# Four layers on one core: how the scan of Layer 0 gets its B and C, from four products with eightfold weights or from two products and a copy through DRAM

## The chip, the cores and the metric

The kernel runs on one core of a Trainium2 chip. The metric is the time of the device in microseconds (us). All values are 32-bit floats.

## The reference

The input x has 8 images of 128 channels and 64 x 64 positions. Four layers follow each other, each of the form x = x + f(group_norm(x)). Only Layer 0 is touched. It treats the lower 64 channels with a selective scan over the 4096 positions of an image (DI = 128 inner channels d, N = 16 states n, R = 4) and the upper 64 with a 3 x 3 convolution:

```python
xc = silu(conv1d(xs))                         # xs, z = layer_norm(t) @ in_w
dbc = xc @ xproj_w                            # 4 + 16 + 16 columns
dt = softplus(dbc[..., :R] @ dt_w + dt_b)
Bm = dbc[..., R:R + N]
Cm = dbc[..., R + N:]
dA = exp(dt[..., None] * A)
dBx = dt[..., None] * Bm[:, :, None, :] * xc[..., None]
h = dA_t * h + dBx_t                          # the scan, for each d and n
y = einsum('bdn,bn->bd', h, C_t)              # then y * silu(z) @ out_w, and x_hw's convolution beside it
```

Layer 1 sends rows over the image with a 9-tap convolution in four directions, each row depending on the one before. Layer 2 is three small convolutions, Layer 3 a deformable convolution with gathers.

## The kernel before

**Tiling of the scan.** For the scan a partition holds one pair (d, n): 8 channels d times 16 states n are 128 partitions. An image is cut into 4 chunks of 1024 positions (NCK), so there are 32 chunks in all, and each chunk into two halves h of T = 512. A half has 16 groups of 8 channels, taken two at a time, which makes 8 scan steps in a half, 16 in a chunk and 512 in all. In a step i (main loop, L639 on, with `where` L558):

- TensorE spreads u = dt * xc to the (d, n) partitions of the next step (`step_u`, `spread`, L568, bank u_ps) and dt, times A, for the step after it (`step_dt`, L568, bank dt_ps).
- ScalarE takes the exponential, the decay da (`step_decay`, L585).
- VectorE multiplies u_ps with B, which is tile bc[:, 0] (`step_scan`, L592), and scans twice (L603).
- ScalarE saves the last column (`step_carry`, L609), and GpSimd multiplies with C, tile bc[:, 1], in place (`step_weigh`, L614).
- In every odd step TensorE sums over n into ps_y (`round_sum`, L622), for the two steps three and two back. hb has four buffers, so a scan in an even step needs that sum of the step before.

**B and C.** Each (d, n) partition needs B or C of its n, the same for all eight d. `bc_product` (L446) gets this from TensorE directly: the weights w_bc (made once, L247) repeat the 16 columns of xproj_w eight times, so a product of 128 x 512 leaves B (i = 0) or C (i = 1) of one half on all 128 partitions, and ScalarE copies it into bc (L453). That is four products and four copies in a chunk. The tile bc has two buffers, one of a half each.

**Order of the work.** The schedule is written out by hand: every engine runs its instructions in the order in which the program issues them. The other work of a chunk c is planned in `plan_chunk` as events at step numbers relative to t0 = 16 c (L524 to L555). The steps below are counted modulo 16; an event can belong to the chunk before or after.

| step | events with work on TensorE (through the one bank "g" of `ps_g`) | other events |
|---|---|---|
| 0, 1 | xs_product (L395, three taps) | x_st load (even steps, in one chunk of four) |
| 2, 3 | bc_product (i = 0, 1) of half 1, then z_product (L407) | y_gate (step 2), silu (step 3, L412, with a table load before and after), x_o loads |
| 4 | y_product (L492, L494; evicted at L496) | |
| 5, 6 | v_product (L422) | normalize (step 5, L357), out_add with the x1d store, v_exp (step 6) |
| 7 | t_product (L365) | v_round (L430) |
| 8 | t_var (L373) | out_stats (L514) |
| 9 | | v_log |
| 10, 11 | bc_product of half 0 | v_sum and y_gate (step 10) |
| 12 to 15 | conv_taps (L477) | v_sum (step 14), load of xr (step 15) |

`ps_g` has one bank, so a product there waits until ScalarE has read the one before. SP issues nearly all loads and stores, in program order; it runs ahead of the steps until one of its transfers has to wait. In one chunk of four the group norms of an image are worked out as well (`norm_product`, L281 and L289, at steps 4 and 12).

**Layer 1 beside Layer 0.** The first four images go through Layer 1 while Layer 0 works on the last four: from step 280 on, the second of the two u_ps banks is given to Layer 1 (`shared`, L575), and from step 294 on each step also carries one row of it: nine taps on TensorE (L733, `layer1.products`) and one VectorE instruction (L741, `layer1.add`). After step 511 Layer 1 goes on alone, and Layers 2 and 3 follow.

Of the kernel before, what the change touches and what calls it, by code (L numbers as in the profile page):

```python
# [10 lines left out]
F32 = mybir.dt.float32  # L11
# [6 lines left out]
P = 128  # L18
# [4 lines left out]
GC, D, DI, N, R, KC = 64, 64, 128, 16, 4, 3  # L23
T = 512
# [10 lines left out]
def conv_preact_kernel(ctx: ExitStack, tc: tile.TileContext, a: dict, out: bass.AP):  # L35
    nc = tc.nc
    x_in = a["x"].rearrange("b c h w -> b c (h w)")
# [3 lines left out]
    dram = ctx.enter_context(tc.tile_pool(name="dram", bufs=1, space=DRAM))  # L41


    ident = const.tile([P, P], F32, name="ident")
    make_identity(nc, ident)

    gmat = const.tile([P, P], F32, name="gmat")
# [13 lines left out]
    x1d = [dram.tile([C, HW], F32, name=f"x1d{b}") for b in range(B)]  # L61
# [2 lines left out]
    x3d = [dram.tile([C, HW], F32, name=f"x3d{b}") for b in range(B)]  # L64
    tables = [dram.tile([SIDE * SX, 2 * C], F32, name=f"table{b}") for b in range(B)]


    norm1 = const.tile([P, B, 2], F32, name="norm1")

# [5 lines left out]
    xp = ctx.enter_context(tc.tile_pool(name="x", bufs=1))  # L75
    w1 = ctx.enter_context(tc.tile_pool(name="l1", bufs=2))
    X = xp.tile([P, HW, NB2], F32, name="X")
    layer0(tc, a, ident, gmat, x_in, x1d, norm1, Layer1First(tc, a, w1, x1d, norm1, X))

    with tc.tile_pool(name="l2w", bufs=1) as wp, tc.tile_pool(name="l2", bufs=2) as w2, tc.tile_pool(  # L80
        name="l3", bufs=2
    ) as w3, tc.tile_pool(name="l12ps", bufs=1, space=PSUM) as p2, tc.tile_pool(
        name="l3ps", bufs=2, space=PSUM
# [15 lines left out]
        N = two.TICKS  # L99
# [22 lines left out]
        for n in range(min(plans), (B + 1) * N):  # L122
            b, i = n // N - 1, n % N
# [19 lines left out]
    finish(tc, a, eps, od, x3d, y_out, st, const)  # L143


def layer0(tc, a, ident, gmat, x_in, x1d, norm1, layer1):

# [2 lines left out]
    nc = tc.nc  # L152
# [3 lines left out]
    with ExitStack() as ctx:  # L156
        wp = ctx.enter_context(tc.tile_pool(name="l0w", bufs=1))
        w2 = ctx.enter_context(tc.tile_pool(name="l0", bufs=2))
# [7 lines left out]
        def load(name, shape, *parts):  # L166
            t = wp.tile(shape, F32, name=name)
            for sl, src in parts:
                nc.sync.dma_start(t[sl], src)
            return t  # L170

        ALL, LO, HI = slice(0, P), slice(0, 64), slice(64, P)
# [4 lines left out]
        xproj_w = load("xproj_w", [DI, R + 2 * N], (ALL, a["xproj_w"]))  # L177
# [4 lines left out]
        ln_b = load("ln_b", [P, 1], *both(a["ln_b"]))  # L182
        in_b = load("in_b", [DI, 2], (ALL, a["in_b"]))
        c1_w = load("c1_w", [DI, KC], (ALL, a["conv1d_w"]))
        c1_rows = load("c1_rows", [P, KC * DI], (ALL, a["conv1d_rows"].to_broadcast([P, KC * DI])))
        c1_b = load("c1_b", [DI, 1], (ALL, a["conv1d_b"]))
        dt_b = load("dt_b", [DI, 1], (ALL, a["dt_b"]))
        d_ssm = load("d_ssm", [DI, 1], (ALL, a["D_ssm"]))
# [5 lines left out]
        with tc.manual_schedule():  # L194
# [5 lines left out]
            def ps_g(name):  # L200
                return pg.tile([P, T], F32, tag="g", name=name)
# [7 lines left out]
            ps = ps_g("ps_ec")  # L209
# [8 lines left out]
            ps = ps_g("ps_cb")  # L218
# [5 lines left out]
            ps = ps_g("ps_ib")  # L224
# [17 lines left out]
            ps = ps_g("ps_dt")  # L242
            nc.tensor.matmul(ps[:, 0:DI], lhsT=xdt_t, rhs=dt_w, start=True, stop=True)
            w_dt = wp.tile([DI, DI], F32, name="w_dt")
            nc.vector.tensor_copy(w_dt, ps[:, 0:DI])

            w_bc = wp.tile([DI, 2, 8, N], F32, name="w_bc")  # L247
            for i in range(2):
                nc.vector.tensor_copy(
                    w_bc[:, i], xproj_w[:, R + i * N : R + (i + 1) * N].unsqueeze(1).to_broadcast([DI, 8, N])  # L250
                )

            nc.scalar.activation(a_neg, a_neg, AF.Exp)
            nc.vector.tensor_scalar_mul(a_neg, a_neg, -1.0)
# [56 lines left out]
            def at(when, what):  # L311
                events.setdefault(when, []).append(what)
# [25 lines left out]
            def plan_chunk(c):  # L338
                b, g = c // NCK, c % NCK
                r0 = g * CR  # L340
                t0 = 16 * c
                s = S[c] = {}
# [100 lines left out]
                    nc.gpsimd.tensor_add(dt, w, s["rv"][:, h])  # L443
                    nc.gpsimd.tensor_mul(u, dt, s["xc"][:, h])

                def bc_product(i, h):  # L446
                    if i == 0:
                        s["bc", h] = w2.tile([P, 2, T], F32, name="bc")
                    ps = ps_g("ps_bc")
                    nc.tensor.matmul(  # L450
                        ps, lhsT=w_bc[:, i].rearrange("p d n -> p (d n)"), rhs=s["xc"][:, h], start=True, stop=True
                    )
                    nc.scalar.copy(s["bc", h][:, i], ps)  # L453

                def y_gate(h):
                    y = s["y", h] = w2.tile([DI, T], F32, name="y")
# [64 lines left out]
                def also(f, *args):  # L521
                    return lambda: f(*args)
# [10 lines left out]
                for h in range(2):  # L533
                    at(t0 - 16 + h, also(xs_product, h))
                    at(t0 - 14 + h, also(z_product, h))
                    at(t0 - 11 + h, also(v_product, h))
                    at(t0 - 6 + 4 * h, also(v_sum, h))
                    for i in range(2):
                        at(t0 - 6 + 8 * h + i, also(bc_product, i, h))
                    at(t0 + 10 + 8 * h, also(y_gate, h))  # L540
                    at(t0 + 11 + 8 * h, also(y_mul, h))
                at(t0 - 13, silu)
                at(t0 - 10, v_exp)
                at(t0 - 9, v_round)
                at(t0 - 8, v_rest)
# [88 lines left out]
            for c in range(total):  # L634
                plan_chunk(c)
                if c % NCK == 0:
                    plan_stats(c // NCK, 16 * c - 64)
# [641 lines left out]
```

## Time and profile before

| | |
|---|---|
| runs | 7735.23, 7738.29, 7739.29 us; median 7738.29 us |
| profiled execution, its own time | 7708.51 us |
| its span, first to last instruction | 7706.8 us |
| mean granted TensorE clock | 0.903 |
| busy: TensorE, VectorE, ScalarE, GpSimd | 81%, 58%, 45%, 52% of the span |
| L450 products of B and C | 256 records (two for a call), median 697 ns, overlapping |
| L453 copies | 128, median 586 ns |
| scan steps (L592), first and last start | 96.0 and 3101.8 us |

The profile is that of one execution, and each line of a timeline gives the start in us, the duration in us, the engine, the line of the kernel, the operation, the tiles (written <- read), the shapes and how many instructions were merged into the line. In brackets stands how long the engine was idle before it and what released it. A 32-bit matrix product appears as two records, each pair of them one call. PE is TensorE, DVE VectorE, ACT ScalarE, POOL GpSimd. In a row of the view of windows, each engine has its busy us and the number of instructions in brackets; PEclk is the granted TensorE clock as a share of full speed.

### The profile page before, as it was taken

What the parts mean: (1) busy time and instruction counts of PE and PEld (TensorE: products, weight loads), DVE (VectorE), ACT (ScalarE), POOL (GpSimd) and SP (SyncE); (2) the same over time, 40 slices, a digit from 0 to 9 for tenths busy, and PEclk for the clock granted to TensorE, in tenths of its full rate; (3) what the DMA queues carried; (4) which work ended last, traced back from release to release, by engine and by line L of the source; (5) the groups of instructions that cost most, each with busy time, mean ns of one, the idle gap of its engine ahead of it and who ended that gap; (6) DMA issues with size and microseconds to landing.
All of it is one profiled execution on the core that took longest, in us unless ns stands there. A gap on an engine that the chain in (4) does not pass through costs nothing.

```text
span 7706.8 us, 87506 instructions
## 1 busy us (share of the span) xinstructions
PE 6228.2 (81%) x30574; PEld 4062.3 (53%) x30574; DVE 4497.4 (58%) x5332; ACT 3460.5 (45%) x8218; POOL 4009.0 (52%) x3261
## 2 busy tenths in 40 slices
PE   6888878799999999859898898986678777776661
PEld 1222222255555556637677777775555555555550
DVE  4888889666566566141265666657545454555445
ACT  4555656433333332020155445455455555555552
POOL 3767777444444444000155555456566666666664
PEclk9988889699999999979999999998889888988785
DMA  1011111000000000041255556567666666666667
GB/s 43 27 38 36 39 34 38 31 11 27 12 29 21 9 15 15 12 157 29 66 182 183 166 174 192 167 186 253 204 210 202 208 194 208 201 206 203 186 185 264
DMA packets 333017, 897.81 MB, mean 116 GB/s; under 512 B 55464, under 2 KB 90544, under 8 KB 330528
## 3 DMA queue, kind: packets, MB, share of 16 engines
q0 software_dynamic: 184320, 604.13, 26.0%
q1 hardware_dynamic: 143648, 271.31, 10.6%
q10 hardware_dynamic: 4608, 16.78, 0.5%
q8 instruction: 242, 3.96, 0.2%
q14 instruction: 199, 1.63, 0.1%
HBM read 770.80 MB, written 121.21 MB: 116 GB/s over the span
## 4 chain that ended last, share of the span: by engine, by line
PE 62%; ACT 12%; DVE 8%; issue 8%; another core or an unknown queue 5%; DMA 3%; POOL 2%; SPq 0%; DVEq 0%; POOLq 0%; ACTq 0%
PE u_ps L733 13%; PE ps_l L733 10%; PE ps_s L1155 8%; PE ps_o L1166 6%; PE u_ps L568 5%; ACT X L1134 4%; PE ps_c L477 3%; PE ps_t L894 3%; DVE hb L603 3%; PE ps_y L622 3%; PE ps_x L395 3%; PE ps_t L908 2%; ACT samp L1106 1%; PE ps_off L990 1%
## 5 line engine op out<-in xcount | busy, mean ns | idle before, releaser
L614 POOL TENSOR_TENSOR hb<-hb,bc 128x1024 f32<-128x1024 f32 x512 | 1217.2, 2385 | 1279.7 <-ACT carry L609 893.5
L1123 POOL DMA_INDIRECT X<-table,idx x1386 | 1315.4, 949 | 788.4 <-issue 304.4
L1123 POOL DMA_INDIRECT got<-table,idx x918 | 878.6, 957 | 1351.4 <-DVE idx L1046 545.9
L603 DVE TENSOR_TENSOR_SCAN hb<-da,carry,u_ps 128x512 f32<-128x512 f32 x896 | 1097.8, 1266 | 251.0 <-PE ps_y L622 178.5
L585 ACT ACTIVATE da<-dt_ps 128x1024 f32<-128x1024 f32 x512 | 524.3, 1024 | 1337.7 <-PE dt_ps L568 1337.0
L1155 PE MATMUL ps_s<-ident,X 128*128 128x128 f32 x5544 | 829.7, 308 | 268.0 <-issue 175.7
L1141 DVE TENSOR_TENSOR X<-prod,X 128x768 f32<-128x768 f32 x462 | 442.4, 958 | 916.7 <-ACT X L1134 706.6
L1155 PEld LDWEIGHTS ps_s<-ident,X 128*128 128x128 f32 x5544 | 794.6, 221 | 339.3 <-issue 212.2
L1134 ACT ACTIVATE X<-X,wgt 128x128 f32<-128x128 f32 x2772 | 860.5, 394 | 0.0
L1166 PE MATMUL ps_o<-samp,dcn_w 128*128 128x256 f32 x2304 | 646.3, 422 | 225.3 <-ACT samp L1106 140.5
L568 PE MATMUL u_ps<-u,m_u 32*128 32x512 f32 x2048 | 629.6, 693 | 152.7 <-DVE hb L603 152.5
L1106 ACT COPY samp<-ps_s 128x384 f32<-128x384 f32 x768 | 360.9, 470 | 796.7 <-remote 479.9
L592 DVE TENSOR_TENSOR u_ps<-u_ps,bc 128x1024 f32<-128x1024 f32 x512 | 624.7, 1220 | 153.8 <-PE dt_ps L568 136.9
L568 PE MATMUL dt_ps<-dt,m_dt 32*128 32x512 f32 x2048 | 631.6, 695 | 17.5 <-ACT da L585 17.4
L1166 PEld LDWEIGHTS ps_o<-samp,dcn_w 128*128 128x128 f32 x2304 | 464.6, 212 | 332.9 <-ACT samp L1106 159.6
L1134 ACT ACTIVATE got<-got,wgt 128x128 f32<-128x128 f32 x1836 | 569.5, 393 | 0.0
L1139 DVE TENSOR_TENSOR prod<-X,prod 128x768 f32<-128x768 f32 x462 | 443.6, 960 | 100.6 <-ACT prod L1113 47.1
L741 DVE SCALAR_TENSOR_TENSOR X<-ps_l,X 128x256 f32<-128x256 f32 x252 | 106.2, 421 | 620.3 <-PE ps_l L733 473.4
L568 PEld LDWEIGHTS u_ps<-u,m_u 32*128 32x128 f32 x2048 | 164.8, 196 | 510.0 <-DVE hb L603 311.1
L741 DVE SCALAR_TENSOR_TENSOR X<-u_ps,X 128x256 f32<-128x256 f32 x252 | 106.9, 424 | 501.7 <-PE u_ps L733 501.3
L894 PE MATMUL ps_t<-xn,w 128*128 128x512 f32 (+4 forms) x688 | 305.2, 592 | 54.8 <-ACT t L901 22.5
L1155 PE MATMUL ps_s<-ident,got 128*128 128x128 f32 x2076 | 294.0, 287 | 38.2 <-issue 28.6
(227 smaller groups left out, 10393.2 us busy)
## 6 DMA issues: line engine op xcount, KB each, us to landing
table<-tok SPq DMA_DIRECT2D x128, 256.0 KB
x<-x1d SPq DMA_DIRECT2D x96, 256.0 KB
X<-table,idx POOLq DMA_INDIRECT x1386
x<-x2d SPq DMA_DIRECT2D x48, 384.0 KB
x3h<-x3d SPq DMA_DIRECT2D x16, 1056.0 KB
x_st<-in_x SPq DMA_DIRECT2D x64, 256.0 KB
x_o<-in_x SPq DMA_DIRECT2D x64, 256.0 KB
x1d<-res SPq DMA_DIRECT2D x64, 256.0 KB
```

The source lines that it names most:

```text
L568: nc.tensor.matmul(ps[:, j, :], lhsT=mask[q, r].rearrange("p d n -> p (d n)"), rhs=S[c][src, h][q, :], start=True, stop=True,)
L585: nc.scalar.activation(da, steps[i]["dt"], AF.Exp)
L592: nc.vector.tensor_mul(st["bc"], st["bc"], s["bc", h][:, 0].unsqueeze(1).to_broadcast([P, 2, T]))
L603: nc.vector.tensor_tensor_scan(hb[:, j, :], st["da"][:, j, :], st["bc"][:, j, :], start, ALU.mult, ALU.add)
L614: nc.gpsimd.tensor_mul(hb, hb, S[c]["bc", h][:, 1].unsqueeze(1).to_broadcast([P, 2, T]))
L733: nc.tensor.matmul(ps[:, c0:c1, :], lhsT=w[:, k, :], rhs=v[:, prev, c0 + k - PAD : c1 + k - PAD, :], start=(k == PAD), stop=(k == K - 1),)
L894: nc.tensor.matmul(ps[:, o0 - a0 : o1 - a0, :], lhsT=self.w1[:, k, :], rhs=S["xn", g][:, i0 + o0 : i0 + o1, :], start=(k == 2), stop=(k == 4),
L1123: nc.gpsimd.indirect_dma_start(out=got[:, k, :, :].rearrange("p q c -> p (q c)"), out_offset=None, in_=tab, in_offset=bass.IndirectOffsetO ...
L1134: nc.scalar.activation(got[:, k, q, :], got[:, k, q, :], AF.Identity, scale=wgt[:, t, k0 + k, q : q + 1])
L1139: nc.vector.tensor_mul(prod, got[:, :, 0:2, :], w.unsqueeze(3).to_broadcast([P, G3, 2, C]))
L1155: nc.tensor.matmul(ps[:, k, :], lhsT=got[:, k, q, :], rhs=self.ident, start=(q == 0), stop=(q == halves - 1))
L1166: nc.tensor.matmul(ps, lhsT=self.dcn_w[:, k, :], rhs=samp[:, k - k0, :], start=(k == 0), stop=(k == KK - 1))
```

## The change

B and C of both halves of a chunk are computed once on 64 partitions (half, B or C, n): two products with the 32 plain columns of xproj_w, into partitions 0 to 31 and 32 to 63 of one bank, then one copy to a tile bc_n. SP writes that tile to DRAM (bcd, two buffers in turn), and for each half eight transfers, one for each d, read 32 rows of 512 values from there into 16 partitions of bc. The products move from steps 10, 11 (half 0) and 2, 3 (half 1) to step 7; the transfers are issued at steps 10 and 2. The weights w_bc are gone, and the tile c1_rows, used only while weights are prepared, now lives in the buffer of xz.

```diff
+    bcd = [dram.tile([P // 2, T], F32, name=f"bcd{i}") for i in range(2)]
...
-        c1_rows = load("c1_rows", [P, KC * DI], (ALL, a["conv1d_rows"].to_broadcast([P, KC * DI])))
+        c1_rows = w2.tile([P, KC * DI], F32, tag="xz", name="c1_rows", bufs=1)
+        nc.sync.dma_start(c1_rows, a["conv1d_rows"].to_broadcast([P, KC * DI]))
...
-            w_bc = wp.tile([DI, 2, 8, N], F32, name="w_bc")
-            for i in range(2):
-                nc.vector.tensor_copy(
-                    w_bc[:, i], xproj_w[:, R + i * N : R + (i + 1) * N].unsqueeze(1).to_broadcast([DI, 8, N])
-                )
...
-                def bc_product(i, h):
-                    if i == 0:
-                        s["bc", h] = w2.tile([P, 2, T], F32, name="bc")
+                def bc_product():
                     ps = ps_g("ps_bc")
-                    nc.tensor.matmul(
-                        ps, lhsT=w_bc[:, i].rearrange("p d n -> p (d n)"), rhs=s["xc"][:, h], start=True, stop=True
-                    )
-                    nc.scalar.copy(s["bc", h][:, i], ps)
+                    for h in range(2):
+                        nc.tensor.matmul(
+                            ps[32 * h : 32 * h + 32], lhsT=xproj_w[:, R:], rhs=s["xc"][:, h], start=True, stop=True
+                        )
+                    bc = w2.tile([2 * 2 * N, T], F32, name="bc_n", bufs=1)
+                    nc.scalar.copy(bc, ps[0 : 2 * 2 * N])
+                    nc.sync.dma_start(bcd[c % 2], bc)
+
+                def bc_spread(h):
+                    bc = s["bc", h] = w2.tile([P, 2, T], F32, name="bc")
+                    for d in range(8):
+                        nc.sync.dma_start(
+                            bc[16 * d : 16 * d + 16],
+                            bcd[c % 2][32 * h : 32 * h + 32, :].rearrange("(i n) t -> n i t", n=N),
+                        )
...
-                    for i in range(2):
-                        at(t0 - 6 + 8 * h + i, also(bc_product, i, h))
+                    at(t0 - 6 + 8 * h, also(bc_spread, h))
...
+                at(t0 - 9, bc_product)
```

## Prediction

> **What bounds the kernel now.** The change touches only the first layer, so I first read the view of windows, 200 us each, over the first 4200 us. The layer's scan steps run from 96.0 to 3101.8 us (first and last start of the VectorE product L592 in the view of tile bc). They fall into two regimes, one row of each:
>
> ```profile
> core 0: us, PE busy (x) PEld busy (x) DVE busy (x) ACT busy (x) POOL busy (x), PEclk, DMA share, GB/s
> 1000.00:1200.00 200.00, 156.00 (x691) 40.77 (x689) 172.14 (x158) 118.48 (x176) 134.26 (x69) 0.87 0.14 45
> 2200.00:2400.00 200.00, 191.18 (x916) 114.91 (x915) 125.05 (x136) 72.08 (x111) 84.21 (x45) 0.97 0.08 26
> ```
>
> In the first (steps 0 to 279) VectorE is the busiest, 172 of 200 us, and TensorE idles a fifth of the time. In the second (from step 294, when Layer 1's rows are woven in) TensorE is busy 191 of 200 us and VectorE 125. DMA engines are busy a tenth in both.
>
> Then the timeline of TensorE in the second regime, steps 9 and 10 of one chunk:
>
> ```profile
> 2259.80 0.70 PE L568 MATMUL u_ps<-u,m_u 32*128 32x512 f32 x2
> ...
> 2260.87 1.06 PE L622 MATMUL ps_y<-hb,m_y 128*32 128x512 f32 x8
> 2261.87 4.02 PE L733 MATMUL u_ps<-X,w_up 128*128 128x256 f32 x18
> 2265.82 0.70 PE L568 MATMUL u_ps<-u,m_u 32*128 32x512 f32 x2
> ...
> 2266.89 1.12 PE L450 MATMUL ps_bc<-act,w_bc 128*128 128x512 f32 x2
> 2267.85 3.92 PE L733 MATMUL u_ps<-X,w_up 128*128 128x256 f32 x18
> 2271.70 0.70 PE L568 MATMUL u_ps<-u,m_u 32*128 32x512 f32 x2
> ```
>
> Nothing stands between the rows: a step there is the sum of its TensorE work. Measuring from u_ps to u_ps over 12 chunks of this view (median) gives step 2 7.93 us, step 3 8.87, step 6 5.88, step 7 7.02, step 10 5.88, step 11 7.07 (step 9 6.02, step 8 5.88); 118.0 us for the 16. One 512-column product costs about 1.0, and a step with no extra product would take 4.88.
>
> The product of B or C is dearer where another product follows it through the one bank "g" of PSUM, as in steps 2 and 3:
>
> ```profile
> 2211.19 1.12 PE L450 MATMUL ps_bc<-act,w_bc 128*128 128x512 f32 x2
> 2211.41 1.02 ACT L585 ACTIVATE da<-dt_ps 128x1024 f32<-128x1024 f32 x1 [5.36 <-PE dt_ps L568]
> 2212.41 0.59 ACT L453 COPY bc<-ps_bc 128x512 f32<-128x512 f32 x1
> 2213.05 1.12 PE L407 MATMUL ps_z<-q,in_w 64*128 64x512 f32 x2 [0.73 <-ACT bc L453]
> ```
>
> From L450's start to L407's start is 1.86 us: the product and a wait for the copy, which itself stands behind the exponential L585.
>
> In the first regime I read the timeline of VectorE from one L592 to the next. In chunks without statistics of a batch (8 of 15 chunks from step 32 on) VectorE idles about 3.0 us of some 68: 1.1 in step 2, 0.9 in step 4, 1.7 in step 6, nothing elsewhere, nothing in steps 3, 10, 11. The idle of step 6 comes like this:
>
> ```profile
> 1010.78 1.28 ACT L412 ACT_TABLE_LOAD   x1
> 1012.07 1.91 ACT L412 ACTIVATE act<-xz 128x2048 f32<-128x2048 f32 x1
> 1014.00 1.28 ACT L413 ACT_TABLE_LOAD   x1
> 1015.39 1.02 ACT L585 ACTIVATE da<-dt_ps 128x1024 f32<-128x1024 f32 x1
> ...
> 1016.46 1.13 PE L568 MATMUL dt_ps<-dt,m_dt 32*128 32x512 f32 x4 [1.35 <-ACT da L585]
> 1017.74 2.00 PE L422 MATMUL ps_v<-act,w_dt 128*128 128x512 f32 x2 [0.15 <-ACT res L496]
> ...
> 1021.71 2.33 DVE L603 TENSOR_TENSOR_SCAN hb<-da,u_ps 128x512 f32<-128x512 f32 x2 [1.40 <-PE ps_y L622]
> ```
>
> ScalarE's silu with its two table loads (4.5 us) holds up the decay L585, that holds up the bank dt_ps, that TensorE, and that the sum L622, which frees the buffer of the scan.
>
> [...] the four calls (eight records) of L622 on 32-column tiles take 1.06 us, one call of L450 1.12. [...] Here the first x_st load is issued at 15.7 us and read at 22.1, so 256 KB land within 6.4 us.
>
> **The change, part by part.** Second regime first, chunks 19 to 31, 13 of them, all with TensorE as the sum.
> - Steps 10 and 11 lose one product each: 5.88 - 4.88 = 1.00 and 7.07 - 6.02 = 1.05. In step 10 VectorE idles 1.09 us today, so TensorE stays the longer one only just; I count 0.9.
> - Step 2 loses product and wait: it becomes a step with one product, 7.93 - 5.88 = 2.05. Step 3 becomes what step 7 is now (one product and L622): 8.87 - 7.02 = 1.85.
> - Step 7 gains the new product ahead of ps_t. Two calls on two column tiles take the time of one (about 1.06, from L622), the copy waits for the same exponential, ps_t waits for the copy: it becomes what step 3 is now, +1.85. The lower bound is 1.0, if the wait is hidden; the upper 2.9, if the two calls don't overlap.
> - Sum: 0.9 + 1.05 + 2.05 + 1.85 - 1.85 = 4.0 us a chunk, 52 us in 13.
>
> First regime, about 17 chunks. Removing products in steps 10 and 11 gives nothing, VectorE has no idle there. Removing them in steps 2 and 3 brings silu forward: 3.66 us of TensorE and 1.2 us of ScalarE (two copies at 0.59) go. Re-running the timeline above by hand, with u_ps held only by the end of the scan before, silu starts about 3.1 us earlier, the decay ends at 1013.3 instead of 1016.4, L622 at 1017 instead of 1021, before VectorE asks at 1020. So the idle of steps 4 and 6 goes (0.9 + 1.7 = 2.6 at most); that of step 2, behind the three-tap products of steps 0 and 1, stays. Step 7 gains 1.86 us on TensorE: from the end of scan 6 TensorE then needs 1.1 + 1.86 + 1.05 + 1.06 = 5.1, VectorE until scan 8 needs 1.21 + 2.33 + 1.46 (L430) + 1.21 = 6.2, so it is covered; at the half clock of L422 (2.00) it would not be and costs up to 3. Chunks with statistics have longer idles (8.7 to 10.8 us), one kind of them behind the eviction L496 that follows silu, so they gain as much. Bounds 0 and 2.6 a chunk; I take 1.8, 31 us in 17. Between the regimes (steps 280 to 293) u_ps has one bank and TensorE waits for each scan: nothing.
>
> The 17 new transfers a chunk go to SP's queue. SP takes 0.33 to 0.38 us for an issue (x_st, x_o), so 6.5 us of a 75 us chunk. The traffic is 64 + 512 rows of 2 KB; q1 needed 10.6% of 16 x 7706.8 us for 143648 packets, 91 ns each, so 3.3 us a chunk on 16 engines. Waits: the write of bcd waits in step 7 for its copy; behind it stand x_st loads that have three steps until they are read. The spreads wait for that write and for the last weighing L614 of the buffer's former half, in steps 8 and 0; behind them stand x_o, x_st and xr, each used three or more steps later. From there a spread has six steps at least, 6 x 4.7 = 28 us, and needs 8 x 0.38 + at most 6.4 = 9.5 us. Hidden; if not, see below. VectorE and GpSimd may each take more wait instructions (17 ns each on ScalarE's queue at L453): 16 a chunk, 0.3 us, 30 chunks, 0 to 9 us; I take 2. Moving c1_rows and dropping w_bc act once, before 96 us: under 1 us.
>
> Sum: -52 - 31 + 2, about -81. Against the profiled execution's 7708.5 us that is 7627.5; the median of the runs, 7738.3, stands 0.4% higher, and I carry the difference over: about 7657.5 us.
>
> **The rivals.**
> - *Only the second regime gains.* The wait at step 7 or the clock takes back the first regime's share: TensorE is busy less there, and L422 already ran at half speed after a wait. For it: VectorE is busy 86%. Then -52 + 2, and a little lost at step 10: 7690 us.
> - *The spreads arrive late (slower).* One mechanism: the scan's product L592 at steps 0 and 8 waits for eight transfers behind SP's waits. It costs only beyond 28 us from release to landing, three times my estimate. Each us beyond costs 34 halves in the first regime, so from 2.4 us beyond (3.8 us for each of the eight in a row) the gain of 81 is gone; at 5 us beyond, -81 + 170: 7827 us. Against it: idle queues, rows of 2 KB.
> - *Nothing moves.* The copies' end, not the products, paces both regimes, and step 7 takes all of it: 7738 us. Against it: back-to-back rows in regime two.
> - *More than counted.* Chunks with statistics shed more of their 9 us: -110, 7628 us.
>
> **How the numbers follow.** Forecast 0.58 (7635 to 7680), only the second regime 0.24 (7680 to 7715), spreads late 0.10, nothing 0.04, more than counted 0.04. The range 7630 to 7715 takes in the first two with the bounds of their terms. This kernel can be told from no change by about 0.2%, 15 us: faster 0.86, same 0.04, slower 0.10.
>
> **What would show it.** Right: in regime two steps 2, 3, 10 and 11 near 5.9, 7.0, 5.0 and 6.0 us and step 7 near 8.9, chunk near 114; in regime one no wait for ps_y at steps 4 and 6; L592 never waiting for bc's transfers. Wrong: idle before L592 or L614 released by a DMA, step 8 waiting for ps_y, the new product taking 2 us, or a lower granted clock before 1400 us.

## The result, and the profile after

The changed kernel takes 7711.36 us (median of 22 runs, 7687.67 to 7759.4), the kernel before 7738.79 us (22 runs, 7725.6 to 7753.36): ratio of the means 0.9971, 95% interval 0.9958 to 0.9984, 22 us less (the medians differ by 27). Two repetitions later gave 0.9973 and 0.9974; the first of them leaves out two slow runs, more than 1.5% above its fastest. The forecast was 81 us less. The spread between runs more than doubled, from 28 to 72 us, and the longer a run takes, the lower is its mean granted clock as a rule: 0.898 in the fastest of the 22, 0.887 in the slowest, with a correlation of time and clock of -0.88.

The profiled execution of the changed kernel took 7727.32 us, span 7725.6: longer than the profiled one of before, not shorter. The first layer explains none of that: its last L599 (the former L592) starts at 3078.9 us instead of 3101.8, 23 us earlier, and Layer 1's last row beside it ends 23 us earlier too. What comes later, where not one line differs, took 42 us more in this execution. The change does not slow those later layers: in the ten profiles taken on chips where before takes 7214 to 7220 us, the time after the last scan is 4106 to 4120 us, whichever the kernel; on the others it varies from 4605 to 4658 and is longest with a kernel that has the old products (before_norm). So I compare the first layer by its profiles and the whole by the ratios.

The same two windows as before, now of the changed kernel:

```profile
core 0: us, PE busy (x) PEld busy (x) DVE busy (x) ACT busy (x) POOL busy (x), PEclk, DMA share, GB/s
1000.00:1200.00 200.00, 149.56 (x688) 39.15 (x684) 174.94 (x161) 116.82 (x173) 136.31 (x71) 0.85 0.19 62
2200.00:2400.00 200.00, 188.72 (x909) 113.39 (x906) 131.53 (x138) 69.41 (x106) 88.97 (x47) 0.95 0.11 34
```

TensorE is busy less and VectorE more in both, as forecast; the DMA share has gone up by a few hundredths.

**Where the sums held.** TensorE's timeline in the second regime of the changed kernel, steps 6 and 7 of chunk 23:

```profile
2115.26 0.70 PE L575 MATMUL u_ps<-u,m_u 32*128 32x512 f32 x2
...
2116.33 1.12 PE L419 MATMUL ps_v<-act,w_dt 128*128 128x512 f32 x2
2117.29 3.92 PE L740 MATMUL u_ps<-X,w_up 128*128 128x256 f32 x18
2121.14 0.70 PE L575 MATMUL u_ps<-u,m_u 32*128 32x512 f32 x2
...
2122.21 1.05 PE L447 MATMUL ps_bc<-act,xproj_w 128*32 128x512 f32 x4
2123.94 1.08 PE L362 MATMUL ps_t<-xn,ecc 64*64 64x512 f32 x4 [0.68 <-ACT bc_n L451]
2124.94 1.06 PE L629 MATMUL ps_y<-hb,m_y 128*32 128x512 f32 x8
2125.94 4.02 PE L740 MATMUL u_ps<-X,w_up 128*128 128x256 f32 x18
2129.89 0.70 PE L575 MATMUL u_ps<-u,m_u 32*128 32x512 f32 x2
```

The two calls of L447 together take 1.05 us, the wait for their copy is where it was expected, and step 7 takes 2129.89 - 2121.14 = 8.75 us. Measured the same way, steps 2, 3, 10 and 11 take 6.07, 7.07, 5.05 and 6.02 us, and a chunk without statistics 111.7 us instead of 115.5.

In the first regime the stall behind silu has gone, too. VectorE from step 4 to step 7 of chunk 6:

```profile
557.20 2.45 DVE L610 TENSOR_TENSOR_SCAN hb<-da,carry,u_ps 128x512 f32<-128x512 f32 x2
559.57 1.21 DVE L599 TENSOR_TENSOR u_ps<-u_ps,bc 128x1024 f32<-128x1024 f32 x1
560.91 2.45 DVE L610 TENSOR_TENSOR_SCAN hb<-da,carry,u_ps 128x512 f32<-128x512 f32 x2
563.28 2.39 DVE L354 TENSOR_SCALAR xn<-xr,gm,rs 128x1088 f32<-128x1088 f32 x1
565.59 1.22 DVE L599 TENSOR_TENSOR u_ps<-u_ps,bc 128x1024 f32<-128x1024 f32 x1
566.94 2.45 DVE L610 TENSOR_TENSOR_SCAN hb<-da,carry,u_ps 128x512 f32<-128x512 f32 x2
```

No row carries a bracket: VectorE waits for nothing in steps 4 to 6. Such chunks take 65 to 67 us where they took 68.

**Where they did not.** I then measured each chunk from its first L599 to the next chunk's, in both profiles. Two groups are *longer* than before: chunks 9, 10 and 17 of the first regime (by 13.1, 10.1 and 10.9 us) and chunks 20, 24 and 28 of the second (by 2.3, 3.8 and 4.1 us). All others are shorter or equal, but for chunk 13 (1.8 longer). The sums of the differences: first regime -28.6 us in 15 chunks, +34.1 in three; second regime -36.4 in ten (18 to 30 without the three), +10.2 in three. That makes -21, against -23 for the last L599.

In chunk 9, around step 14, the timeline of the changed kernel has

```profile
836.38 3.62 PE L484 MATMUL ps_c<-xn,conv 64*64 64x504 f32 x8
...
839.93 1.93 PE L629 MATMUL ps_y<-hb,m_y 128*32 128x512 f32 x8
...
842.06 2.45 DVE L610 TENSOR_TENSOR_SCAN hb<-da,carry,u_ps 128x512 f32<-128x512 f32 x2 [4.35 <-PE ps_y L629]
```

and the window over the stretch

```profile
836.00:872.00 36.00, 36.00 (x100) 9.03 (x100) 15.91 (x14) 14.44 (x21) 14.03 (x9) 0.50 0.16 51
```

TensorE is busy all of the 36 us, and its granted clock is 0.50: L629 takes 1.93 us instead of 1.06, and VectorE, which needs its sum, waits 4.35. TensorE at half clock has become the bound, for most of a chunk. The clock records of this trace count 442 us at half clock between 100 and 1400 us, three of the stretches over 50 us long; before, 314 us and none over 35. Both kernels have a further long one at the change of regimes, from 1439 and 1448 us on.

In chunk 20, step 12 (18.9 us, before 12.8), where the group norm of an image is worked out:

```profile
1794.49 4.64 POOL L621 TENSOR_TENSOR hb<-hb,bc 128x1024 f32<-128x1024 f32 x2
...
1794.81 2.04 DVE L281 TENSOR_TENSOR n_dm<-mv,norm 128x1 f32<-128x1 f32 x1
...
1796.88 2.26 DVE L282 SCALAR_TENSOR_TENSOR n_dm<-n_dm,mv 128x1 f32<-128x1 f32 x1
1799.20 0.58 PE L286 MATMUL ps_gv<-n_dm,gmat 128*128 128x1 f32 x2 [4.62 <-DVE n_dm L282]
...
1800.03 5.36 PE L484 MATMUL ps_c<-xn,conv 64*64 64x512 f32 x12 [0.25 <-DVE n_dm L287]
1805.32 6.77 PE L740 MATMUL u_ps<-X,w_down 128*128 128x256 f32 x18
```

Before, in this step:

```profile
1800.39 0.16 DVE L284 TENSOR_TENSOR n_dm<-mv,norm 128x1 f32<-128x1 f32 x1
1800.59 0.22 DVE L285 SCALAR_TENSOR_TENSOR n_dm<-n_dm,mv 128x1 f32<-128x1 f32 x1
1800.86 0.38 PE L289 MATMUL ps_gv<-n_dm,gmat 128*128 128x1 f32 x2 [0.70 <-DVE n_dm L285]
1801.10 2.36 POOL L614 TENSOR_TENSOR hb<-hb,bc 128x1024 f32<-128x1024 f32 x1 [0.59 <-ACT carry L609]
```

Two instructions on one column, which work out n_dm for the group norm, take 2.04 and 2.26 us instead of 0.16 and 0.22. Each ends when one of the two multiplications of GpSimd, 2.36 us each, is over. The two lines make 32 instructions in the changed kernel: 28 are long (0.82 to 2.26 us, the other four 0.16 and 0.22), and each of the 28 starts while a GpSimd instruction on two tensors is running and ends within 0.02 us of the end of that one. In before it is 22 of 32 (0.42 to 2.26 us), so the collision is not new; its places have moved, here into chunks 20, 24 and 28. What in the chip couples the two engines is not shown. In before, GpSimd started its next multiplication at 1801.10, after the pair. TensorE idles 4.62 us instead of 0.70 and then runs 13.7 us at half clock instead of 6.8 (L740 takes 6.77 us, in other steps 4.02).

### The profile page after: what moved, and what is told of

It is laid out like the page before. It is cut to its first block, busy times and chain, and to the rows that moved or that the text cites. A ratio compares the mean times of both kernels' runs of the same rounds, so it can differ in the third digit from the quotient of the medians.

```text
span 7725.6 us, 88211 instructions
## 1 busy us (share of the span) xinstructions
PE 6194.9 (80%) x30446; PEld 4055.3 (52%) x30446; DVE 4498.5 (58%) x5330; ACT 3410.8 (44%) x8122; POOL 3995.6 (52%) x3261
## 4 chain that ended last, share of the span: by engine, by line
PE 57%; ACT 9%; issue 7%; DVE 6%; another core or an unknown queue 5%; DMA 3%; POOL 1%; SPq 0%; DVEq 0%; POOLq 0%; ACTq 0%
PE u_ps L740 13%; PE ps_l L740 11%; PE ps_s L1162 8%; PE ps_o L1173 6%; PE u_ps L575 4%; ACT X L1141 4%; PE ps_t L901 3%; PE ps_c L484 3%; PE ps_y L629 2%; DVE hb L610 2%; PE ps_x L392 2%; PE ps_t L915 1%; PE ps_off L997 1%; ACT samp L1113 1%
## 5 line engine op out<-in xcount | busy, mean ns | idle before, releaser
L621 POOL TENSOR_TENSOR hb<-hb,bc 128x1024 f32<-128x1024 f32 x512 | 1203.5, 2357 | 1262.6 <-ACT carry L616 774.6
L592 ACT ACTIVATE da<-dt_ps 128x1024 f32<-128x1024 f32 x512 | 524.2, 1024 | 1409.9 <-PE dt_ps L575 1409.1
L575 PE MATMUL u_ps<-u,m_u 32*128 32x512 f32 x2048 | 659.5, 724 | 214.4 <-DVE hb L610 214.0
L599 DVE TENSOR_TENSOR u_ps<-u_ps,bc 128x1024 f32<-128x1024 f32 x512 | 625.2, 1221 | 168.7 <-PE dt_ps L575 151.3
L575 PE MATMUL dt_ps<-dt,m_dt 32*128 32x512 f32 x2048 | 661.6, 726 | 7.9 <-POOL dt L440 5.7
L484 PE MATMUL ps_c<-xn,conv 64*64 64x504 f32 (+3 forms) x1152 | 327.6, 693 | 1.8 <-DVE n_dm L287 1.8
```

The costliest lines, as they stand in the source:

```text
L484: nc.tensor.matmul(s["ps_c"].rearrange("p (r w) -> p r w", w=W)[sl, o0:o1, c0:c1], lhsT=conv[HI, k, :], rhs=s["xn"][HI, 1 + 8 * h + o0 + d ...
L575: nc.tensor.matmul(ps[:, j, :], lhsT=mask[q, r].rearrange("p d n -> p (d n)"), rhs=S[c][src, h][q, :], start=True, stop=True,)
L592: nc.scalar.activation(da, steps[i]["dt"], AF.Exp)
L599: nc.vector.tensor_mul(st["bc"], st["bc"], s["bc", h][:, 0].unsqueeze(1).to_broadcast([P, 2, T]))
L621: nc.gpsimd.tensor_mul(hb, hb, S[c]["bc", h][:, 1].unsqueeze(1).to_broadcast([P, 2, T]))
```

## The experiments

Two theories for the loss, taken at first as separate causes: **the clock** (TensorE, with less work, stays at half clock for longer in the first regime) and **the collision** (n_dm meets GpSimd). The rival is that the spreads arrive late or that something else about the transfers costs. Ratios are to the kernel before on the same chip. Three of the four groups ran on chips where before takes 7214 to 7220 us and not 7739 to 7741; in the profiles taken there the first layer takes as long as elsewhere (with no_dma the last scan starts at 3076.6 us), so I carry ratios across chips only roughly.

### n_dm on ScalarE

```diff
-                nc.vector.tensor_sub(dm[:, 0:1], mv[:, 0:1], gm)
-                nc.vector.scalar_tensor_tensor(
-                    dm[:, 1:2], dm[:, 0:1], dm[:, 0:1], mv[:, 1:2], ALU.mult, ALU.add
-                )
+                nc.scalar.activation(dm[:, 0:1], gm, AF.Square, bias=mv[:, 0:1], scale=-1.0)
+                nc.scalar.activation(dm[:, 1:2], dm[:, 0:1], AF.Identity, bias=mv[:, 1:2])
```

> Changed kernel, with the two small VectorE instructions of Layer 0's norm_product (n_dm) done on ScalarE instead. Theory 'collision' (in the second regime the new timing puts them beside a GpSimd multiplication, they take 2.0 and 2.3 us instead of 0.2 each, TensorE idles 4.6 us and falls to half clock): step 12 of chunks 20, 24 and 28 goes from 18.9 us to 12 or less, these chunks from about 122 to 115 us, and some stalls of the first regime go too: 20 to 45 us less than the changed kernel's 7711, about 7680. Rival 'clock alone' (the half clock there would come anyway): chunks 20, 24, 28 stay near 122, time 7711.

Measured: 0.9888 (0.9864 to 0.9911), 81 us below before and so some 60 below the changed kernel, more than expected. The same place of chunk 20:

```profile
1757.22 4.67 POOL L619 TENSOR_TENSOR hb<-hb,bc 128x1024 f32<-128x1024 f32 x2
...
1758.00 0.29 ACT L281 ACTIVATE n_dm<-norm,mv 128x1 f32<-128x1 f32 x1
1758.32 0.29 ACT L282 ACTIVATE n_dm<-n_dm,mv 128x1 f32<-128x1 f32 x1
...
1758.67 0.38 PE L284 MATMUL ps_gv<-n_dm,gmat 128*128 128x1 f32 x2 [1.34 <-ACT n_dm L282]
...
1759.30 5.29 PE L482 MATMUL ps_c<-xn,conv 64*64 64x512 f32 x12 [0.25 <-DVE n_dm L285]
```

GpSimd is at the same work, and TensorE's wait is 1.34 us instead of 4.62. Step 12 takes 15.1, 13.4 and 13.4 us in the three chunks (18.9, 18.7, 17.3), the chunks 119.1, 117.4 and 117.4. The collision theory holds, but not to the 12 us for the step and the 115 for the chunk that I expected: L482 still falls to half clock (5.29 us, where L477 in chunk 24 of before takes 2.79), after a wait of 1.3 us. Against the changed kernel's profile the second regime gains 21.6 us, the first 37; the first regime gave more than I had counted for it.

> Kernel before, with its two small n_dm instructions moved from VectorE to ScalarE as in norm_act. Theory 'collision': before met GpSimd in the first regime and in chunks 21 and 25, not in 20, 24 and 28; so it gains there, some 30 us in all, and chunks 20, 24 and 28 stay within 2 us of 121, 119 and 117: ratio to before 0.995 to 0.997, so norm_act keeps at least 0.993 against it. Rival 'the edit helps both alike': ratio 0.989 or 0.991, and the change of this study is worth no more with it than without.

Measured: 0.9962 (0.9951 to 0.9973). Chunks 20, 24 and 28 take 117.9, 119.5 and 121.2 us, together 2 more than before, but 20 is 3 less and 28 4 more, outside the 2 us that I had expected; 21 and 25 get shorter by 2.3 and 3.4, the first regime by 37. In the main as the theory said: before had its collisions elsewhere. Part of norm_act's gain belongs to before as well: against before_norm, norm_act is 53 us faster by the ratios, and in the two profiles the second regime is 44.7 us shorter and the first 5.3 longer. So with the collision gone the change gave, in these two executions, most of its share of the second regime and nothing in the first.

### Work given back to TensorE

```diff
+                def fill():
+                    ps = ps_g("ps_fill")
+                    nc.tensor.matmul(ps, lhsT=w_dt, rhs=s["xc"][:, 0], start=True, stop=True)
...
+                if c < 18:
+                    for i in (-6, -5):
+                        at(t0 + i, fill)
```

> Changed kernel, with two idle products of 128x128 by 512 (results never read, no copy) at steps 10 and 11 of chunks 0 to 17, where before had its products for half 0. Theory 'clock' (with less work TensorE stays at half clock for longer in the first regime): half-clock time between 100 and 1400 us falls from 442 towards the 314 of before, chunks 9, 10 and 17 lose their 11 to 13 us, total 20 to 35 us less than the changed kernel, about 7685, although there is more work. Rival 'late transfers' (chunks 9, 10 and 17 wait for DMA): the three chunks stay as they are, time 7711 or a few us more.

Measured: 0.9927 (0.9915 to 0.9939): an added, useless product in two steps of a chunk makes the kernel faster, 34 us against the ratio 0.9974 of the repetition after_third. The last scan starts at 3049.5 us, 29 earlier than with the changed kernel alone. The windows from 100 to 1400 us, of before, of the changed kernel and of this one:

```profile
100.00:1400.00 1300.00, 1064.92 (x4686) 279.42 (x4684) 1126.70 (x1012) 732.61 (x1115) 926.40 (x483) 0.88 0.10 34
```

```profile
100.00:1400.00 1300.00, 1047.41 (x4598) 270.70 (x4594) 1119.10 (x1009) 699.97 (x1055) 918.53 (x481) 0.83 0.15 49
```

```profile
100.00:1400.00 1300.00, 1060.03 (x4746) 277.05 (x4742) 1144.18 (x1032) 714.15 (x1076) 934.55 (x489) 0.88 0.17 50
```

The clock comes back to 0.88, which is what before has there, with the transfers unchanged (DMA share 0.17); VectorE gets 25 us more of its work done. Half-clock time is 313 us; one long stretch remains, in chunk 13.

> Changed kernel, with the idle products of fill_10_11 at steps 2 and 3 instead, where before had those of half 1. Theory 'clock': if any added work helps, as fill_10_11, 20 to 35 us less; if only work just ahead of the convolution's taps (steps 12 to 15) helps, no gain, 7711. Rival 'late transfers': 7711 or some us more.

Measured: 0.9993 (0.9979 to 1.0007), half-clock time 465 us, last scan 3110.9. A miss for "any work helps", and by the middle value worse than no filler: at steps 2 and 3 the products push silu back by some 1.8 us, and the clock stays down all the same (chunks 6, 7, 13 and 17 are long). Ahead of the convolution's taps the filler works, here it doesn't.

> As fill_10_11, but the idle products use 32 of the 128 weight columns: the same 512 columns of data and the same duration, a quarter of the array. If TensorE's clock follows the time in which it is busy, as fill_10_11: half-clock time near 313 us between 100 and 1400, ratio 0.993. If it follows how much of the array works, as the changed kernel: near 440 us and ratio 0.997 or more.

Measured: 0.9949 (0.9931 to 0.9966), half-clock time 345 us, last scan 3057.0. Between the two: about half of fill_10_11's gain, with an interval that overlaps both fill_10_11's and that of the repetitions. How much of the help comes from the busy time and how much from the width of the array is left open.

> Kernel before with the two idle products of fill_10_11 at steps 10 and 11 of chunks 0 to 17, beside its own products there. If the filler helps by replacing work that the change took away: no gain here, ratio 0.999 to 1.002. If any such filler helps: ratio 0.996 or less.

Measured: 1.0052 (1.0040 to 1.0065). Slower, and by more than the 1.002 that I had allowed: the filler is no remedy for any kernel. Its products stand behind before's own in the one bank "g" here, and half-clock time is 384 us, more than before's 314, so more work on TensorE does not by itself mean less time at half clock.

Long stretches, counted over all profiles, tell the kernels apart more clearly than sums of half-clock time (norm_act has 419 us of it, and yet its first regime gained 37 us). I count those of over 50 us that begin in chunks 0 to 16. Seven profiles are of kernels with the new products in the first regime, n_dm on VectorE and no filler at steps 10 and 11 (the changed kernel three times, no_dma, fill_2_3, first_only, first_again): 16 stretches, at least one in each. norm_act has one. The five profiles with the old products there have one in all (second_norm), the three with the filler at steps 10 and 11 one in all. And all 19 begin at two places: 13 in step 12 of chunk 4, 8, 12 or 16, where TensorE waits for the group norm (2.85 and 3.40 us in chunk 8 of the changed kernel), six in step 9 or 10 of the chunk after. So in the first regime the two theories meet: the stretches begin at or just after the chain with the collision, and they last mostly where the change has taken work from TensorE and nothing fills it. The wait alone doesn't do it, since before waits there as well (3.5 and 3.0 us in chunk 4) and its longest stretch is 34 us. What makes a stretch last is not shown. Nor do the runs separate the filler's effect on the clock from the shift of some 2 us in a chunk that it gives to the work behind it; that it acts by the clock is read from the records.

### The transfers

```diff
+                    if c:
+                        s["bc", h] = S[0]["bc", h]
+                        return
```

> Changed kernel that leaves out the spreading transfers of all chunks but the first (every chunk uses the B and C of chunk 0); products, copies and the writes to bcd stay. Theory 'clock': the transfers cost nothing, time within 10 us of the changed kernel's 7711, some first-regime chunks still at 78 to 108 us with TensorE at half clock. Rival 'late transfers': chunks 9, 10 and 17 fall to 82, 66 and 82 us, time 35 us less or more, about 7675.

Measured: 0.9956 (0.9938 to 0.9973), half-clock time 444 us, last scan 3076.6 us against 3078.9. Without the spreads chunks 5, 6 and 17 are the long ones (92.3, 82.3 and 94.6 us). So late transfers are not the cause. What they cost is some 13 us by the middle values (0.9956 against 0.9974), and as the intervals overlap it may be nothing.

### Repetition, and both remedies together

> The changed kernel, unaltered, beside the other three of this group. All theories: ratio to before 0.995 to 0.999. Theory 'clock': where its long stretches at half clock lie in the first regime differs from execution to execution, so chunks other than 9, 10 and 17 may be the long ones now, while those of the second regime repeat within 1 us. Rival 'fixed places': the same chunks 9, 10 and 17 are long again.

Measured: 0.9973 (0.9957 to 0.9988). The second regime repeats within 0.3 us in every chunk. In the first, chunks 9 and 10 are long again, 17 is not, 13 and 14 are: where the long stretches fall differs from execution to execution, though not evenly among the chunks. The 22 runs lie between 7655.87 and 7793.54 us.

> Changed kernel with both edits, the idle products at steps 10 and 11 of the first 18 chunks and n_dm on ScalarE. If the two losses are separate causes their gains add, with a little overlap in the first regime: last scan near 2995 us, ratio to before 0.984 to 0.987. If norm_act had already removed what starts the long stretches, the filler adds nothing: ratio 0.988 or 0.989.

Measured: 0.9856 (0.9842 to 0.987), last scan 2986.8 us, 7626.48 us beside 7741.25 for before. The two gains over the changed kernel, 0.0086 and 0.0047, would make 0.984, so they add within the intervals, and this version beats both kernels. Its five runs lie within 20 us. Against before_norm, on the same chip, it is 83 us faster. Not all of that is the first layer's: in the two profiles its last scan starts 74 us earlier (chunks 0 to 17 -24.5, 18 to 30 -47.7), and what comes later, which no edit touches, is 20 us shorter. So with both disturbances reduced, and at the price of the idle products, the change is worth some 74 us.

### The two regimes apart

For the first two the old products are kept in one regime's chunks:

```diff
...
-                    at(t0 - 6 + 8 * h, also(bc_spread, h))
+                    if c < 18:
+                        for i in range(2):
+                            at(t0 - 6 + 8 * h + i, also(bc_direct, i, h))
+                    else:
+                        at(t0 - 6 + 8 * h, also(bc_spread, h))
...
-                at(t0 - 9, bc_product)
+                if c >= 18:
+                    at(t0 - 9, bc_product)
```

This is the edit of second_only, where bc_direct is the old bc_product and w_bc is back; first_only has the two conditions the other way round.

> The change made in chunks 18 to 31 alone, which are the chunks of the second regime; chunks 0 to 17 keep the four products with eightfold weights. Theory 'clock and collision': the second regime brings what it brought in the changed kernel, about 26 us (its own collisions in chunks 20, 24 and 28 stay), the first regime is that of before: ratio 0.996 to 0.997, scatter as small as that of before. Rival 'the first regime gives something of its own on average': this kernel is slower than the changed one's 0.997, ratio near 0.999.

Measured: 0.9953 (0.994 to 0.9966), five runs within 12 us. A little more than expected, and by the middle values more than the whole change gives (0.9974), with intervals that just overlap.

> The change made in chunks 0 to 17 alone. Theory 'clock': what the first regime gains in its undisturbed chunks, 28 us, is given back on average by stretches at half clock: ratio 0.999 to 1.001, scatter several times that of before, half-clock time between 100 and 1400 us over 400. Rival 'the first regime gains': ratio 0.996 or 0.997.

> first_only once more. Theory 'clock takes the first regime's gain back': ratio 0.998 to 1.001 and scatter above that of before. Rival 'it gains': 0.996 or 0.997.

Measured: 0.9984 (0.9966 to 1.0001) and 0.9990 (0.9978 to 1.0001); runs spread over 76 and 69 us where before's spread over 14 and 16. Half-clock time 386 and 427 us (I had expected over 400). In its own profile first_only gained 42 us up to step 272 and lost some at the end; first_again gained 10. On average some 10 us remain of the 31 counted, and as both intervals reach 1 it may be nothing.

> second_only with the two n_dm instructions on ScalarE, as in norm_act and before_norm. If the collisions were what kept the second regime below its 52 us, this kernel lies 45 to 55 us below before_norm's 0.9962: ratio 0.989 to 0.9905. If something else keeps it there, about 26 us below: ratio 0.993.

Measured: 0.991 (0.9891 to 0.9928), 38 us below before_norm by the ratios, between the two numbers; the chunks of its second regime take within 0.3 us what they take in fill_norm, 47 to 48 us less than in before_norm. One chunk of the first regime (9) happened to be long, 92.4 us. The second regime's 52 us are there, less the half clock that step 12 keeps.

> The changed kernel once more, beside first_again on one chip. If the halves add up: ratio 0.994. If the whole suffers more from the clock than its first half alone: 0.997 as before, 10 us or more above the sum of the halves.

Measured: 0.9974 (0.996 to 0.9988). The halves, 0.9953 and some 0.9987, would make 0.994: the whole is about 25 us worse than their sum. No run shows a cause for that, and the intervals leave room for a good part of it to be chance. In the profiled execution, the fastest of the eight, the first regime was little disturbed (half-clock time 388 us, last scan 3046.4), in that of after_again badly disturbed (500 us, 3103.5), so one profile can't decide it; it stays open.

## Why the prediction was wrong, step by step

- **Second regime, per step: right.** Steps 2, 3, 10, 11 and 7 came out at 6.07, 7.07, 5.05, 6.02 and 8.75 us; 3.8 us a plain chunk, counted 4.0. The two calls overlap (1.05 us). Step 10 gave 0.83 of the 0.9 counted.
- **"13 of them, all with TensorE as the sum": wrong.** This is the first failed step. I had taken the gain of the plain chunk and multiplied by 13. The prediction's own numbers held a warning: the medians of the 16 steps add up to 115.5 us, the plain chunk, while its 118.0 is the mean over the 12 chunks; the longer chunks make the difference. In three of the 13 chunks step 12 holds a chain from TensorE to VectorE and back for the group norm, and moving work shifted it onto GpSimd's multiplication. Instead of -12 they brought +10, a difference of 22 us. norm_act shows that the collision is the cause, and second_norm that without it the second regime gives 47.5 of the 52 us. The half-clock part did not go with it: with n_dm on ScalarE step 12 still takes 10 to 15 us.
- **First regime, the stall behind silu: right.** The idle of steps 4 and 6 is gone; 28.6 us in 15 chunks, 1.9 each, counted 1.8. Silu starts 3.0 us earlier in a plain chunk, counted 3.1.
- **First regime, "I take 1.8, 31 us in 17": wrong as a sum.** This is the second failed step: the term for lost clock was put at nothing. Chunks run at half clock took 34 us back in the profiled execution; first_only and first_again say that some 10 us remain on average, if any. I had named the clock, but only as a rival and only for step 7 ("at the half clock of L422 (2.00) it would not be and costs up to 3"). What happened is larger: TensorE at half clock becomes the engine that sets the end, in stretches of more than 50 us, and the steps from 14 of chunk 9 to 2 of chunk 10 take 5 to 10 us, where a step of a plain chunk takes some 4. I priced it as a loss of the 31 us at most, and with a full 52 us in the second regime, so the rival's 7690 us was also short.
- **Transfers: right.** Hidden, at a price of some 13 us by the middle values, and possibly of nothing (no_dma). SP waits once a chunk for the write of bcd before it issues the first spread, 32 times, 1.7 us on average and 2.9 at most; that wait is in its queue alone. A listed sign of being wrong did appear: ten times the view says that a DMA ended GpSimd's idle time before L621, five times one of bc. But each time L621 starts 0.08 to 0.09 us after the end of the copy L616 that it needs anyway, so the copy and not the transfer set its start.
- **The carried sum.** 83 us between before_norm and fill_norm lies close to the 81 forecast, but this is in part luck: in the profiles the first layer gives 74, of which 47.7 in the second regime (counted 52) and 24.5 in the first (counted 31), and fill_norm has idle products that the forecast did not. The terms were sized fairly well; the two disturbances were not in the sum.

## What to carry to other kernels

Taking work from TensorE can cost more than the work is worth: here, in the profiled execution, it brought three stretches of 55 to 58 us at half clock, and the first regime gained 28.6 us and lost 34.1. Look at the granted clock of the stage before counting a saving on TensorE where it is not the bound; in this kernel a wider scatter between runs (72 us instead of 28) was the first sign. A per-step saving multiplied over all periods must be checked on the periods that are different (here every fourth chunk), for what falls beside what after the shift. And a useless product, tried in more than one place, is a cheap way to test whether the clock comes back with the work (here from 0.83 to 0.88, at steps 10 and 11).

## What the runs showed that I had not expected

- TensorE stayed at half clock while it was busy: 36.00 of 36 us at 0.50, within a stretch of 55 us. In those 36 us ran the convolution's taps on 64 x 64 weights, the spreads of u and dt from 32 rows, and the products L392 and L629 between them. That the slowdown is real shows in the products themselves: L629 takes 1.93 us instead of 1.06. Two more full products in a chunk of some 68 us, just before the taps, make the changed kernel faster (0.9927), and fillers at this place leave one long stretch in three profiles; some steps after the end of the taps they don't help (0.9993, three long stretches).
- A wait of TensorE in a busy stretch was often followed by half clock. In step 12 of chunks 20, 24 and 28 the wait of 4.6 us was followed by 10 to 14 us of it in three of three cases (changed kernel), one of 1.34 us by 3 to 10 us in nine of twelve (norm_act, before_norm, second_norm, fill_norm), one of 0.70 us by 3 and 7 us in two of three (before). The waits of 0.68 us before L362 in the same regime (twelve in the changed kernel) were not followed by any, so the length of the wait is not all.
- A one-column VectorE instruction (n_dm, L282) took 2.26 us instead of 0.22 where GpSimd was multiplying, and ended with the multiplication.
